# One timetable for two attention layers: a modulation row used six steps later, three weight fetches spread out, parts of k and q moved back

## The chip, the cores and the metric

The kernel runs on one core of a Trainium2 chip. The core has five engines with a queue each: TensorE (PE: matrix products and transposes, PEld its weight loads), VectorE (DVE), ScalarE (ACT), GpSimd (POOL) and SyncE (SP, which here only starts transfers). Instructions of a queue run in the order in which they were recorded; engines wait for one another by semaphores. Transfers between HBM and the on-chip memory (SBUF) are started from SP's and POOL's queues. The results of products are laid down in PSUM. The metric is the device time of one execution in microseconds (us).

## The reference

Two adaLN layers act on x, 8 batches of 512 tokens with 256 features. `c` gives each layer and batch six rows sa, ca, ga, sb, cb, gb (ga and gb are kept away from zero). Layer 0 has an attention of two branches, linear and windowed, and a feed-forward that mixes each token with the one before. Layer 1 has causal attention with rotary positions (rope) in 16 heads of 16 features, and a gated feed-forward with ternary weights.

```python
x = L0_attn_x
sa, ca, ga, sb, cb, gb = rows(L0_c, L0_wmod)
x = x + ga * L0_attn(layernorm(x) * (1 + ca) + sa)   # [linear | window 64] @ Wout, + its input
x = x + gb * L0_ffn(layernorm(x) * (1 + cb) + sb)    # sigmoid(xr Wr) * (relu(xk Wk)^2 Wv)
sa, ca, ga, sb, cb, gb = rows(L1_c, L1_wmod)
Q, K, V = (layernorm(x) * (1 + ca) + sa) @ w_qkv     # 16 heads of 16
Q, K = rope(Q), rope(K)                              # per head: x*cos + [-x2, x1]*sin
x = x + ga * (softmax(causal(Q K^T / 4)) V @ w_proj + b_proj)
h = layernorm(x) * (1 + cb) + sb
h = silu(w1 h * s1) * (w2 h * s2)                    # 256 -> 1024
h = gelu(h1 h * t1); h = gelu(h2 h * t2)             # 1024 -> 1024, twice
x = x + gb * (w3 h * s3)                             # 1024 -> 256
```

## The kernel before

**One timetable.** The attention of both layers and layer 0's feed-forward are not loops that run one after the other. Every small piece of work is a function that is entered in a list `plan` with a time: `when(time, what)` for layer 0, whose batch b starts at 20b (times after 169 are pressed together by 0.8), and `when1(time, what)` for layer 1, whose batch b starts at 24b; one of its steps is 0.603 of the list's unit once it has got going, and takes 2.33 us on the chip in the steady stretch. At the end the list is sorted by time and its functions are called under a manual schedule. So the order of the instructions on each engine is the order of the times, and nothing moves them afterwards: an instruction that waits holds up all that stands behind it in its queue. Only after the timetable (from 1181 us on) comes layer 1's feed-forward, a loop over the eight batches.

**Layer 1, step by step.** A unit of attention is a batch b, a half c of the features (0 or 1), and a parity e of the heads; a unit has six steps. In a step, `step1` records the scores k, q of one unit (PE, L1102) and the weights qs, k of the unit eight steps behind it (PE, L1160), interleaved. `finish_step1` records what follows: the row maxima on DVE (`junk`, L1113), the exponential on ACT (`at`, L1171) and the causal cut on POOL (`affine_select`, L1175). Once a unit, the maxima are transposed (L1136) and added to q as qs (DVE, L1144), the weights are multiplied by the values (L1194), copied (`ys`), transposed (L1210) and divided by their sums. Products that are not scores share two PSUM buffers, `mm`; scores have three, `sc`.

**What prepares a batch** (`prepare1(b)`). The batch's x is fetched, normalised (`normed`: statistics and `better` on DVE, the inverse root `rr` as two ACT instructions L286 and L287, the normalised rows L318), transposed (L986) and modulated into hT by ACT (L993). `rotation` makes k and q for half c: a product (PE L1012), its copy `flat` (ACT L1018), a swap of halves `rot` (DVE L1022), three POOL operations (L1027: rot times sine, flat times cosine, flat plus rot), and `apart` (ACT L1034), which writes the two head parities e of k or q from flat, each with the other parity's lanes zeroed. `values_of` makes the values (PE L1070).

**The fold of ga.** `fold(i)` prepares the output projection of a batch: fold(0) fetches the row ga as `bc`, a tile of 128 x 256, over SP (`mod_rows`, L189) into a pool with one buffer; fold(1) multiplies the projection's weights by it (`wps`, L973) and the row by the bias (`bc`, L974); fold(2) and fold(3) add that to the two halves of x (L977). All four products and sums are POOL's. The results are needed when `project_out(b)` multiplies by wps (PE L1252) at 24b + 42.45 and adds into x (L1262). Before, the folds stand at steps 49, 52, 53, 54 for batch 1, and at 24b + 6.5, 9.5, 10.5, 11.5 from batch 2 on (54.5, 57.5, 58.5, 59.5 for batch 2).

**bring(4)** at step 48.2 closes layer 0's memory, opens the pool of the feed-forward's weights, and fetches wproj, bproj and the scales over SP, and w1T, w2T and w3T, 1 MB each, over POOL's queue (L894), one behind the other. `look(m)` fetches raw halves of the weights (512 KB) over SP at 50 + 6m; DVE tests their low bits 5.6 steps later. 

**Layer 0's last batch.** `finish(b)` ends a batch of layer 0. It normalises x a second time as `hr` (root, `better`, four rows; for the last batch, 7, on ACT), transposes it (PE L741), and runs the small feed-forward (mixing on POOL and DVE, keys L165, `relu` on ACT, `ka` on DVE, L654 the product). At the time when batch 7 does this, layer 1's first units are already under way. Layer 0's own attention uses `at` and `aw` on ACT (L485, L561), selects on POOL (L489, L571), linear values on PE (L614) and copies of them (`ys`, L648).

Of the kernel before, what the change touches and what calls it, by code (L numbers as in the profile page):

```python
# [10 lines left out]
FR = mybir.dt.float32r  # L11
# [6 lines left out]
P = 128  # L18
B, T, D = 8, 512, 256
H, HD = 16, 16  # L20
NTB = T // P
NC = D // P
NG = 4
DH = 1024
NF = DH // P
# [5 lines left out]
def bcast(ap, shape, axis):  # L31
    return ap.unsqueeze(axis).to_broadcast(list(shape))
# [3 lines left out]
def adaln_two_layers_kernel(ctx: ExitStack, tc: tile.TileContext, t, out):  # L36
    nc = tc.nc
# [3 lines left out]
    def load(pool, name, shape, src, eng=None):  # L41
        dst = pool.tile(list(shape), FP, name=name, tag=name)
        (eng or nc.sync).dma_start(out=dst, in_=src)
        return dst
# [141 lines left out]
    def mod_rows(pool, b, first, n, bufs=2):  # L186

        bc = pool.tile([P, n, D], FP, name="bc", tag="bc", bufs=bufs)
        nc.sync.dma_start(out=bc, in_=mod_dram[b, first : first + n, :].partition_broadcast(P))  # L189
        return bc  # L190
# [4 lines left out]
    with ExitStack() as lctx:  # L195
# [43 lines left out]
        for h0 in (0, 64):  # L239
            first, later = wmask[h0 : h0 + 64, 0, :], wmask[h0 : h0 + 64, 1, :]  # L240
            nc.gpsimd.affine_select(
                out=first, in_=first, pattern=[[-1, P]], compare_op=ALU.is_ge, fill=-1e30, base=0, channel_multiplier=1
            )
            nc.gpsimd.affine_select(
                out=later, in_=later, pattern=[[-1, P]], compare_op=ALU.is_ge, fill=-1e30, base=WIN, channel_multiplier=1
            )
            nc.gpsimd.affine_select(
                out=later, in_=later, pattern=[[1, P]], compare_op=ALU.is_ge, fill=-1e30, base=0, channel_multiplier=-1
# [25 lines left out]
        def when(time, what):  # L274
            plan.append((min(time, END0) + STEP0 * max(time - END0, 0.0), len(plan), what))

        def when1(time, what):
            slow = min(max(time, 0.0), END1)
            plan.append((20 * B + 0.6 + slow + STEP1 * (time - slow), len(plan), what))
# [397 lines left out]
        def finish(b):  # L677

            t0 = 20 * b
# [43 lines left out]
            for j, ats_ in ((0, (34.6, 34.95)), (2, (35.45, 35.85))):  # L723
# [5 lines left out]
                when,  # L729
                lambda: xs0[b],  # L730
                [t0 + i for i in (35.6, 35.8, 36.28, 36.29)],
                t0 + 36.5,
                [t0 + 37.4 + 0.15 * j for j in range(NTB)],
                "hr",
                b == B - 1,
            )
# [100 lines left out]
        for m in range(2 * B):  # L837
            t0 = 10 * m
# [13 lines left out]
        for b in range(B):  # L852
            prepare(b)
            finish(b)
# [5 lines left out]
        def bring(i):  # L860
            if i == 0:
                got1["wqkv"] = wp.tile([P, NC, 3 * D], FP, name="wqkv", tag="wqkv")
                nc.sync.dma_start(out=got1["wqkv"], in_=t["L1_attn_w_qkv"].rearrange("(k p) n -> p k n", p=P))
            elif i == 1:
                got1["rope"] = fm.tile([P, 2, T], FP, name="rope", tag="qm", bufs=2)
                nc.sync.dma_start(out=got1["rope"][:, 0, :], in_=t["rope_cos"])
                nc.sync.dma_start(out=got1["rope"][:, 1, :], in_=t["rope_sin"])
            elif i == 2:


                cmask = got1["cmask"] = fm.tile([P, T], FP, name="cmask", tag="cat0", bufs=2)
                nc.gpsimd.memset(cmask, 0.0)
                diag = cmask[:, T - P : T]
                nc.gpsimd.affine_select(
                    out=diag, in_=diag, pattern=[[-1, P]], compare_op=ALU.is_ge, fill=-4e9, base=0, channel_multiplier=1
                )
            elif i == 3:

                home = [rp.tile([P, 2, T], FP, name="home", tag="aw", bufs=4) for _ in range(2)]
                got1["wproj"], wps[0] = (home[0][:, i, :].rearrange("p (k n) -> p k n", k=NC) for i in range(2))  # L880
                got1["bproj"], got1["bc"] = (home[1][:, 0, i * D : (i + 1) * D] for i in range(2))
                nc.sync.dma_start(out=got1["wproj"], in_=w_proj)
                nc.sync.dma_start(out=got1["bproj"], in_=t["L1_attn_b_proj"].partition_broadcast(P))
                nc.sync.dma_start(out=got1["bc"], in_=mod_dram[0, 4, :].partition_broadcast(P))
            else:
                only0.close()
                fpool = ctx.enter_context(tc.tile_pool(name="ffn_w", bufs=1, side="right"))
                lp = got1["lp"] = only1.enter_context(tc.tile_pool(name="only1", bufs=1, side="right"))
                got1["wproj"] = load(lp, "wproj", [P, NC, D], w_proj)
                got1["bproj"] = load(lp, "bproj", [P, D], t["L1_attn_b_proj"].partition_broadcast(P))  # L890

                for name, n, cols in (("w1T", NC, DH), ("w2T", NC, DH), ("w3T", NF, D)):
                    dst = full[name] = fpool.tile([P, n, cols], FR, name=name, tag=name)
                    nc.gpsimd.dma_start(out=dst, in_=t[name].rearrange("(k p) n -> p k n", p=P))  # L894
                for name in ("w1_s_cols", "w2_s_cols", "h1_s_cols", "h2_s_cols"):
                    full[name] = load(fpool, name, [P, NF], t[name])
                full["w3_s"] = load(fpool, "w3_s", [P, D], t["L1_ffn_w3_s"].partition_broadcast(P))
                full["x0"] = fpool.tile([P, NTB, D], FP, name="x0", tag="x0")
                full["low"] = fpool.tile([P, 22], FP, name="low", tag="low")
                full["flag"] = fpool.tile([1, 1], I32, name="flag", tag="flag")  # L900

        w_proj = t["L1_attn_w_proj"].rearrange("(k p) n -> p k n", p=P)
        only1, full = ExitStack(), {}
        for i, at in enumerate((146.2, 150.0, 157.0, 171.5)):
            when(at, lambda i=i: bring(i))
        when1(48.2, lambda: bring(4))


        raws = [
# [29 lines left out]
        def prepare1(b):  # L939

            t0 = 24 * b
# [24 lines left out]
            def fold(i):  # L966
                if i == 0:
                    held["bc"] = mod_rows(got1["lp"], b, 4, 1, 1)[:, 0, :] if b else got1["bc"]
                    if b:
                        wps[b] = got1["lp"].tile([P, NC, D], FP, name="wps", tag="wps", bufs=2)  # L970
                elif i == 1:
                    bc = held["bc"]
                    nc.gpsimd.tensor_tensor(wps[b], got1["wproj"], bcast(bc, [P, NC, D], 1), ALU.mult)  # L973
                    nc.gpsimd.tensor_tensor(bc, bc, got1["bproj"], ALU.mult)  # L974
                else:
                    h = xs1[b][:, 2 * i - 4 : 2 * i - 2, :]
                    nc.gpsimd.tensor_tensor(h, h, bcast(held["bc"], [P, 2, D], 1), ALU.add)  # L977

            at = (31.0, 49.0)[b] if b < 2 else t0 + 6.5
            for i in range(4):  # L980
                when1(at + (0.0, 3.0, 4.0, 5.0)[i], lambda i=i: fold(i))

            def by_features(c):
                ps = mm.tile([P, T], FP, name="mm", tag="mm")
# [67 lines left out]
            for c, which, at, begin, then, turn, last in (  # L1052
                (0, "k", -11.55, 152.50, 153.0, (153.3, 153.6, 154.2, 154.8), (156.0, 156.3)),
                (0, "q", -8.55, 153.50, 154.1, (155.0, 155.4, 156.0, 156.6), (157.9, 158.2)),
                (1, "k", 0.45, 156.70, 157.2, (157.5, 158.0, 158.6, 159.2), (160.3, 160.8)),
                (1, "q", 3.45, 157.70, 158.3, (159.9, 160.2, 160.8, 161.4), (162.2, 162.7)),
            ):
                if b == 0:
                    rotation(c, which, when, (begin, begin), then, turn, last)
                else:  # L1060
                    at += t0
                    turn = [at + i for i in (2.1, 2.4, 3.3, 4.2)]
                    near = b == 1 and at < 30.0
                    rotation(c, which, when1, (at, at + (0.05 if near else 1)), at + (0.5 if near else 1.6), turn, (at + 5.3, at + 6.1))
# [17 lines left out]
            for j, at in ((0, t0 + 6.45), (2, t0 + 9.45)):  # L1082
                if b == 0:
                    at = (6.7, 8.7)[j // 2]
# [219 lines left out]
        for b in range(B):  # L1304
            prepare1(b)
            project_out(b)
            for m in range(3 * b, min(3 * b + 3, len(raws))):
                at = 50 + 6 * m
                when1(at, lambda m=m: look(m))
                for i in range(2):  # L1310
                    when1(at + 5.6 + i, lambda m=m, i=i: low_bits(m, i))
# [212 lines left out]
```

## Time and profile before

| what | value |
|---|---|
| time, 3 runs | 1867.52 us median (1866.74 to 1873.74) |
| profiled execution | 1871.11 us, its span 1869.4 us |
| mean granted PE clock | 0.976 |
| PE busy | 1765.4 us, 94% |
| DVE busy | 1080.4 us, 58% |
| ACT busy | 895.6 us, 48% |
| POOL busy | 718.0 us, 38% |
| moved by DMA | 65.98 MB, mean 35 GB/s |

The page of the profile shows one execution. Busy shares are averages over stages with different limits. The timetable ends near 1181 us; behind it POOL is almost idle and PE runs the feed-forward's products. A row of the timeline gives the start, the duration, the engine, the line, the operation with its output and inputs and the shapes; the bracket says how long the engine was idle before it and which instruction released it. A row of a stretch gives, for each engine, busy time and the number of instructions, and then the granted clock of PE (1.00 is full speed), the share of DMA time and the rate.

### The profile page before, as it was taken

The page shows a single profiled execution, that of the slowest core. Times are in us where ns is not written, and L with a number is a line of the kernel's source. Part 1 is how long each engine was busy: PE and PEld are TensorE (multiplying, and loading weights), DVE is VectorE, ACT ScalarE, POOL GpSimd, SP SyncE. Part 2 cuts the span into 40 slices and gives each one's busy share as a digit, 9 for nine tenths or more (in the row PEclk, how much of TensorE's full clock was granted, in tenths as well). Part 3 has the DMA queues.
Part 4 walks back from the last instruction along what each step waited for, and adds up shares of the span by engine and source line. Part 5 has one row for each costly group of instructions (what it writes and reads, how often), then busy time and mean ns, then how long its engine had stood idle before and what let it go on. Part 6 is the DMA issues. An engine that isn't in the chain of part 4 may idle for free. (4 is left out here: it accounts for less than half of the span.)

```text
span 1869.4 us, 41160 instructions
## 1 busy us (share of the span) xinstructions
PE 1765.4 (94%) x16878; PEld 1198.6 (64%) x16878; DVE 1080.4 (58%) x3717; ACT 895.6 (48%) x1279; POOL 718.0 (38%) x1094
## 2 busy tenths in 40 slices
PE   3999999999999999989999999799999999999998
PEld 2456566665666654545545544588878888888877
DVE  3555664755646556568888885636363544636352
ACT  1676666766667544556766655322231322223221
POOL 4566856768575753565665653100000000000000
PEclk7999999999999998999999999899999999999999
DMA  4100001010000110042212110600000000000000
GB/s 148 44 2 14 20 24 36 5 36 26 19 18 31 39 31 11 24 108 75 66 49 69 51 49 24 217 0 15 1 26 26 1 26 1 26 1 26 1 15 13
DMA packets 41893, 65.98 MB, mean 35 GB/s; under 512 B 4056, under 2 KB 33368, under 8 KB 41696
## 3 DMA queue, kind: packets, MB, share of 16 engines
q1 hardware_dynamic: 36512, 47.02, 8.0%
q0 software_dynamic: 5184, 16.25, 2.8%
q8 instruction: 134, 2.20, 0.5%
q14 instruction: 63, 0.52, 0.1%
HBM read 50.63 MB, written 12.63 MB: 34 GB/s over the span
## 5 line engine op out<-in xcount | busy, mean ns | idle before, releaser
L1113 DVE CUSTOM_DVE_ANT_0 junk<-sc,cmask 128x256 bf16<-128x256 f32 (+3 forms) x512 | 225.4, 487 | 105.1 <-PE sc L1102 104.6
L1171 ACT ACTIVATE at<-sc 128x768 f32<-128x768 f32 (+1 forms) x192 | 168.9, 882 | 118.9 <-PE sc L1102 104.3
L571 POOL TENSOR_SCALAR_AFFINE_SELECT aw<-aw 64x512 f32<-64x512 f32 (+1 forms) x320 | 167.5, 550 | 101.9 <-ACT aw L561 95.8
L1102 PE MATMUL sc<-k,q 32*128 32x512 f32 (+3 forms) x1024 | 194.7, 477 | 4.9 <-ACT at L1171 4.9
L1370 PE MATMUL mm<-g2h,h 128*128 128x512 f32 x512 | 199.2, 389 | 0.0
L1370 PE MATMUL mm<-g2l,h 128*128 128x512 f32 x512 | 199.2, 389 | 0.0
L485 ACT ACTIVATE at<-sc 128x768 f32<-128x768 f32 (+1 forms) x192 | 164.2, 885 | 66.5 <-PE sc L474 65.9
L1370 PE MATMUL mm<-g1h,h 128*128 128x512 f32 x512 | 194.0, 389 | 0.0
L1370 PE MATMUL mm<-g1l,h 128*128 128x512 f32 x512 | 193.9, 389 | 0.0
L1160 PE MATMUL sc<-qs,k 32*128 32x384 f32 (+3 forms) x1024 | 190.6, 472 | 0.0
L1175 POOL TENSOR_SCALAR_AFFINE_SELECT at<-at 128x256 f32<-128x256 f32 x256 | 102.1, 411 | 193.8 <-ACT at L1171 193.4
L518 DVE CUSTOM_DVE_ANT_0 junk<-sc,wmask 128x128 bf16<-128x128 f32 x512 | 115.3, 286 | 80.4 <-PE sc L507 80.2
L489 POOL TENSOR_SCALAR_AFFINE_SELECT at<-at 128x256 f32<-128x256 f32 x256 | 103.9, 426 | 104.3 <-ACT at L485 103.3
L1427 ACT ACTIVATE row<-mm,h_s_cols 128x512 f32<-128x512 f32 x64 | 44.2, 690 | 188.0 <-PE mm L1370 188.0
L1160 PEld LDWEIGHTS sc<-qs,k 32*128 32x128 f32 x1024 | 82.0, 185 | 67.7 <-DVE maxima L1113 37.2
L1341 DVE CAST g3h<-row 128x512 fp32r<-128x512 f32 x64 | 27.3, 427 | 157.7 <-ACT row L1427 157.7
L1420 ACT ACTIVATE row<-mm,h_s_cols 128x512 f32<-128x512 f32 x64 | 43.5, 689 | 152.4 <-PE mm L1370 152.4
L1414 ACT ACTIVATE sg<-mm,w_s_cols 128x512 f32<-128x512 f32 x64 | 44.2, 691 | 144.8 <-PE mm L1370 88.8
L1370 PEld LDWEIGHTS mm<-g1h,h 128*128 128x128 f32 x512 | 96.1, 188 | 20.2
L1370 PEld LDWEIGHTS mm<-g1l,h 128*128 128x128 f32 x512 | 96.1, 188 | 20.1
L1370 PEld LDWEIGHTS mm<-g2h,h 128*128 128x128 f32 x512 | 96.1, 188 | 20.0
L1370 PEld LDWEIGHTS mm<-g2l,h 128*128 128x128 f32 x512 | 96.1, 188 | 19.9
(223 smaller groups left out, 3970.3 us busy)
## 6 DMA issues: line engine op xcount, KB each, us to landing
x_mid<-x SPq DMA_DIRECT2D x16, 512.0 KB, 3.2
x<-x_mid POOLq DMA_DIRECT2D x9, 512.0 KB, 4.3
x<-in_L_attn_x_dram SPq DMA_DIRECT2D x8, 512.0 KB, 4.5
raw<-in_h1T_dram SPq DMA_DIRECT2D x8, 512.0 KB, 3.5
raw<-in_h2T_dram SPq DMA_DIRECT2D x8, 512.0 KB, 3.5
h<-in_h1T_dram POOLq DMA_DIRECT2D x8, 512.0 KB, 7.7
h<-in_h2T_dram POOLq DMA_DIRECT2D x8, 512.0 KB, 10.0
out_dram<-tmp SPq DMA_DIRECT2D x16, 256.0 KB, 2.2
```

The source lines that it names most:

```text
L485: nc.scalar.activation(at, ps[:, :, :o], AF.Square, scale=0.5)
L489: nc.gpsimd.affine_select(out=d, in_=d, pattern=[[0, 2], [1, P]], compare_op=ALU.is_ge, fill=0.0, base=0, channel_multiplier=-1,)
L518: nc.vector.tensor_tensor_reduce(junk, ps[:, i, ii * P : (ii + 1) * P], wmask[:, int(blk > 0), :], -1.0, BIG, ALU.add, ALU.min, maxima[:, ...
L571: nc.gpsimd.affine_select(out=d, in_=d, pattern=[[0, d.shape[1]], [sign, 64]], compare_op=ALU.is_ge, fill=0.0, base=0, channel_multiplier= ...
L1102: nc.tensor.matmul(ps[:, i, o : o + m], q[r, e, qb * P : (qb + 1) * P], k[r, e, :m], start=True, stop=True,)
L1113: nc.vector.tensor_tensor_reduce(junk[:, :m], ps[:, i, o : o + m], got1["cmask"][:, T - m :], -1.0, BIG, ALU.add, ALU.min, maxima[:, NTB * ...
L1160: nc.tensor.matmul(ps[:, i, o : o + m], k[r, e, kb * P : (kb + 1) * P], qs[r, kb * P : T], start=True, stop=True)
L1171: nc.scalar.activation(at, ps[:, :, :o], AF.Exp, scale=0.25)
L1175: nc.gpsimd.affine_select(out=d, in_=d, pattern=[[0, 2], [1, P]], compare_op=ALU.is_ge, fill=0.0, base=0, channel_multiplier=-1,)
L1370: nc.tensor.matmul(ps, w[:, k, col : col + P], part[:, k, :], start=(k == 0 and i == 0), stop=(k == n - 1 and i == len(parts) - 1),)
L1414: nc.scalar.activation(sg, pa, AF.Silu, scale=full["w1_s_cols"][:, f : f + 1])
L1427: nc.scalar.activation(row(f), ps, AF.Gelu, scale=full["h2_s_cols"][:, f : f + 1])
```

## The change

Four things move in the timetable; no instruction is added or dropped, and PE's order stays as it was.

1. Layer 0's batch 7: its second root moves from 36.5 to 37.0 of its times, and its four normalised rows from 37.4 to 37.6 and following.
2. w1T, w2T and w3T: their buffers are still made in bring(4), but the three transfers are entered singly at steps 62.9, 68.9 and 74.9.
3. Folds: batch 1 still fetches its row at 49 but uses it at 58, 59 and 60; batch 2 fetches at 61 and uses the row at 64, 65 and 66. From batch 3 on nothing changes. On SP the fetch for batch 2 thereby goes behind one raw half of the low-bit test.
4. Layer 1's batch 0, half 1: `apart` of k moves from 160.3 and 160.8 to 161.3 and 162.3, that of q from 162.2 and 162.7 to 163.3 and 164.3. On ACT the two copies ys of layer 0 then come ahead of the k parts, and the q parts fall between relu, aw and the copies of the features.

```diff
--- before.py
+++ after.py
@@ -729,8 +729,8 @@
                 when,
                 lambda: xs0[b],
                 [t0 + i for i in (35.6, 35.8, 36.28, 36.29)],
-                t0 + 36.5,
-                [t0 + 37.4 + 0.15 * j for j in range(NTB)],
+                t0 + (36.5 if b < B - 1 else 37.0),
+                [t0 + (37.4 if b < B - 1 else 37.6) + 0.15 * j for j in range(NTB)],
                 "hr",
                 b == B - 1,
             )
@@ -889,9 +889,8 @@
                 got1["wproj"] = load(lp, "wproj", [P, NC, D], w_proj)
                 got1["bproj"] = load(lp, "bproj", [P, D], t["L1_attn_b_proj"].partition_broadcast(P))
 
-                for name, n, cols in (("w1T", NC, DH), ("w2T", NC, DH), ("w3T", NF, D)):
-                    dst = full[name] = fpool.tile([P, n, cols], FR, name=name, tag=name)
-                    nc.gpsimd.dma_start(out=dst, in_=t[name].rearrange("(k p) n -> p k n", p=P))
+                for i, (name, n, cols) in enumerate((("w1T", NC, DH), ("w2T", NC, DH), ("w3T", NF, D))):
+                    full[name] = fpool.tile([P, n, cols], FR, name=name, tag=name)
                 for name in ("w1_s_cols", "w2_s_cols", "h1_s_cols", "h2_s_cols"):
                     full[name] = load(fpool, name, [P, NF], t[name])
                 full["w3_s"] = load(fpool, "w3_s", [P, D], t["L1_ffn_w3_s"].partition_broadcast(P))
@@ -904,6 +903,11 @@
         for i, at in enumerate((146.2, 150.0, 157.0, 171.5)):
             when(at, lambda i=i: bring(i))
         when1(48.2, lambda: bring(4))
+        for i, name in enumerate(("w1T", "w2T", "w3T")):
+            when1(
+                62.9 + 6 * i,
+                lambda name=name: nc.gpsimd.dma_start(out=full[name], in_=t[name].rearrange("(k p) n -> p k n", p=P)),
+            )
 
 
         raws = [
@@ -976,9 +980,9 @@
                     h = xs1[b][:, 2 * i - 4 : 2 * i - 2, :]
                     nc.gpsimd.tensor_tensor(h, h, bcast(held["bc"], [P, 2, D], 1), ALU.add)
 
-            at = (31.0, 49.0)[b] if b < 2 else t0 + 6.5
+            at = (31.0, 49.0, 61.0)[b] if b < 3 else t0 + 6.5
             for i in range(4):
-                when1(at + (0.0, 3.0, 4.0, 5.0)[i], lambda i=i: fold(i))
+                when1(at + (0.0, 9.0, 10.0, 11.0)[i] if b == 1 else at + (0.0, 3.0, 4.0, 5.0)[i], lambda i=i: fold(i))
 
             def by_features(c):
                 ps = mm.tile([P, T], FP, name="mm", tag="mm")
@@ -1052,8 +1056,8 @@
             for c, which, at, begin, then, turn, last in (
                 (0, "k", -11.55, 152.50, 153.0, (153.3, 153.6, 154.2, 154.8), (156.0, 156.3)),
                 (0, "q", -8.55, 153.50, 154.1, (155.0, 155.4, 156.0, 156.6), (157.9, 158.2)),
-                (1, "k", 0.45, 156.70, 157.2, (157.5, 158.0, 158.6, 159.2), (160.3, 160.8)),
-                (1, "q", 3.45, 157.70, 158.3, (159.9, 160.2, 160.8, 161.4), (162.2, 162.7)),
+                (1, "k", 0.45, 156.70, 157.2, (157.5, 158.0, 158.6, 159.2), (161.3, 162.3)),
+                (1, "q", 3.45, 157.70, 158.3, (159.9, 160.2, 160.8, 161.4), (163.3, 164.3)),
             ):
                 if b == 0:
                     rotation(c, which, when, (begin, begin), then, turn, last)
```

## The prediction

> **What bounds the kernel now.** I read the page's busy shares and chain, then busy time by 20-us stretches, then the timeline where PE falls short, engine by engine. In the page:
>
> ```profile
> span 1869.4 us, 41160 instructions
> PE 1765.4 (94%) x16878; PEld 1198.6 (64%) x16878; DVE 1080.4 (58%) x3717; ACT 895.6 (48%) x1279; POOL 718.0 (38%) x1094
> PE 33%; DVE 1%; DMA 1%; ACT 0%; issue 0%; ACTq 0%; SPq 0%
> ```
>
> PE bounds. The chain followed back covers only the feed-forward from 1181 us, which the change leaves alone, but all stages before it share PE's queue, so time that PE loses before 1181 is lost at the end, and only that time. The stretches with short PE time that touch the change (columns: stretch, sum, PE, PEld, DVE, ACT, POOL, granted clock, DMA share, GB/s):
>
> ```profile
> 640.00:660.00 20.00, 17.29 (x322) 9.97 (x323) 14.48 (x47) 12.04 (x18) 18.03 (x25) 0.94 0.01 2
> 720.00:740.00 20.00, 17.06 (x115) 7.66 (x115) 12.27 (x55) 13.22 (x24) 8.31 (x11) 0.81 0.00 1
> 820.00:840.00 20.00, 14.09 (x112) 7.56 (x104) 8.93 (x38) 8.04 (x11) 13.27 (x16) 0.83 0.68 181
> 840.00:860.00 20.00, 20.00 (x188) 9.97 (x188) 16.20 (x56) 11.84 (x18) 13.11 (x19) 1.00 0.23 65
> ```
>
> At 820 PE lacks 5.9 us and the clock is down, while DMA is at 0.68. The timeline there (start, duration, engine, line, what it waited for):
>
> ```profile
> 816.10 0.93 POOL L894 DMA_DIRECT2D w3T<-in_w3T_dram  x1
> 818.63 0.63 SPq L189 DMA_DIRECT2D bc<-mod_dram  x1
> 829.11 1.26 POOL L973 TENSOR_TENSOR wps<-wproj,bc 128x512 f32<-128x512 f32 x1 [3.64 <-DMA bc<-mod_dram]
> 831.86 1.26 POOL L1027 TENSOR_TENSOR flat<-flat,rot 128x512 f32<-128x512 f32 x1
> 833.16 0.82 ACT L1034 ACTIVATE k<-flat,hot,half 128x512 f32<-128x512 f32 x1 [5.62 <-POOL flat L1027]
> 834.70 2.08 PE L1070 MATMUL mm<-wqkv,hT 128*128 128x256 f32 x4 [5.91 <-ACT hT L993]
> ```
>
> So the row bc lands 10.4 us after its issue, POOL stands in the product wps behind it, the rotation's last addition stands behind that on POOL, `apart` (L1034) on ACT, then the copy hT, and PE.
>
> What an idle stretch of PE does to the clock, in windows of 3.41 us and the two that follow (same columns):
>
> ```profile
> 722.45:725.86 3.41, 2.11 (x14) 1.06 (x12) 3.13 (x13) 1.84 (x4) 1.43 (x2) 0.98 0.00 0
> 725.86:732.69 6.83, 6.83 (x32) 1.92 (x32) 4.48 (x19) 5.74 (x12) 3.38 (x5) 0.51 0.01 2
> 265.06:268.47 3.41, 2.32 (x64) 1.12 (x52) 1.31 (x10) 1.69 (x3) 1.86 (x3) 1.00 0.12 25
> 268.47:275.30 6.83, 6.71 (x113) 3.98 (x106) 5.39 (x22) 5.00 (x9) 4.01 (x6) 1.00 0.05 12
> ```
>
> A window with 62% PE is followed by 6.83 us at half clock, one with 68% is not. Those 6.83 us lose up to half, 3.4 us; between these shares lies the point. The Trainium skill (TensorE: Matmul & The Clock Gate, "Why this matters for your kernels") puts the drop after PE-idle gaps above some 3 us; here a window with 1.30 us of idle time was enough, so the row decides.
>
> **A. First weights out of step 48.2, row of batch 1 used at 58.** Removed from POOL at 814.64 to 817.03: three DMA issues (0.74, 0.74, 0.93). Removed from 829 to 838: wps 1.26, bc 0.72, two additions of 1.27; they go to steps 58 to 60, where the same four of batch 2 now lie (845.59 to 852.41, PE 20.00 of 20 there), so they cost nothing; the row's fetch stays at step 49, nine steps of 2.33 us before its use, twice its 10.4. Without the wait POOL does the two selects from 825.7, the rotated sum from 826.46 to 827.73, ACT k to 828.6 and hT to 829.4, so L1070 starts at 829.45 instead of 834.70: 5.25 us. The half clock of 834.70 to 838.2 goes too: 3.5/2 = 1.75. Sum **-7.0**. Bounds: -5.25 if a drop comes anyway; -7.6 if the 0.67 us left vanishes too.
>
> **D. What comes into its place: batch 2 at 64 to 66.** POOL is nearly full there with batch 3's rotation:
>
> ```profile
> 860.85 0.77 POOL L1175 TENSOR_SCALAR_AFFINE_SELECT at<-at 128x256 f32<-128x256 f32 x2 [0.30 <-ACT at L1171]
> 861.59 1.27 POOL L1027 TENSOR_TENSOR flat<-flat,rot 128x512 f32<-128x512 f32 x1
> 862.89 0.82 ACT L1034 ACTIVATE k<-flat,hot,half 128x512 f32<-128x512 f32 x1 [0.28 <-POOL flat L1027]
> ```
>
> New ahead of 861.59: the issue of w1T (0.74), wps 1.34 and bc 0.68 (start to start at 829.11), less what idle time of POOL takes up; by queueing the rows the sum flat+rot ends at 864.80 instead of 862.86, 1.94 later. ACT's k and the copy aT behind it go 1.96 later, and PE L1252, which at 864.23 already waits 0.36 us for aT, stands 2.3 us. The two additions (1.23 each) delay the next selects; with them PE loses **2.4** in all. A window with 2.3 us idle is past the 1.30 that dropped the clock: a full drop is 3.4, I take 3.0 since PE waits a little in it anyway: **+5.4**. Bounds: 0 (batch 3's rotation slides into POOL's gaps) to 2.4 + 3.4, and with a second stall at q's sum (868.38) 11.2. The fetch of bc at 61 moves on SP behind one raw half; it can start once batch 1's second addition frees its only buffer (852.4), and at the median landing of 3.4 us it is there at 855.8, before wps. The other two weight issues (0.74 and 0.93 on POOL at 68.9 and 74.9) meet gaps of POOL (2.63 idle before 873.11), at most 0.5 of the second in a rotation: 0. On the DMA engines each weight now runs alone; the raw halves of the check are used 5.6 steps, 13 us, after their issue, against 15.6 for the slowest landing in the full pile: 0, at most 0.5. The Trainium skill (DMA: Bandwidth & Descriptors, "Issuing engines are not separate DMA queues") says that transfers of SP and POOL run on the same engines and interleave; the 10.4 against 3.4 agrees.
>
> **B. Second norm of layer 0's last batch.** ACT's order at 720:
>
> ```profile
> 723.99 0.30 ACT L286 ACTIVATE rr<-mv,eps 128x4 f32<-128x4 f32 x1 [3.39 <-DVE mv L305]
> 724.43 1.01 ACT L1171 ACTIVATE at<-sc 128x1024 f32<-128x1024 f32 x1
> 725.49 1.91 PE L1102 MATMUL sc<-k,q 32*128 32x512 f32 x4 [0.98 <-ACT at L1171]
> ```
>
> The root stands ahead of the exponential, whose scores were there at 722.55. Moved behind it (and behind the second k and the other batch's root), the exponential ends 1.88 earlier and PE's 0.98 + 0.32 idle there go. What is late next: on DVE, qs (L1144) now runs at 725.8 to 726.5, ahead of the batch's normalisation; its product on PE waits 1.7 us, so I keep a clock drop. Then hr comes 1 us later (the last at 731.0) and L741 starts at 732.4 instead of 733.32: **-0.9**. Bounds: -4 (second drop of 739.5 gone, 3.1 more) to +1.3, if PE's wait for hr adds a stall of the size removed.
>
> **C. Parts of k and q, second half, batch 0.** ACT's order at 654:
>
> ```profile
> 654.04 1.52 ACT L1034 ACTIVATE k<-flat,hot,half 128x512 f32<-128x512 f32 x2 [4.39 <-POOL flat L1027]
> 655.47 1.05 ACT L648 COPY ys<-mm 128x512 f32<-128x512 f32 x2
> 656.09 3.22 PE L614 MATMUL mm<-at,vo 128*32 128x512 f32 x32 [2.06 <-ACT ys L648]
> ```
>
> The k parts wait for POOL ahead of ys, PE for ys. With ys first it is copied at 651.9 and L614 starts at 654.03: PE's 2.06 go. But POOL is busy without a break from 647 to 664.46, DVE nearly so, and PE then waits for these at 660.9 to 663.1. q's sum still ends at 664.46, relu now waits for it, starts 1.2 us earlier than its 665.74, and the following product at 665.8 instead of 667.68: -1.9 without a clock drop in the new gap, +0.6 with one (2.5 lost, as part of the slow stretch waits for DVE). The gap puts 2.1 idle us into one window, past the 1.30, so I take **+0.6**. Bounds -1.9 to +0.6.
>
> **Sum:** -7.0 + 5.4 - 0.9 + 0.6 = **-1.9**; A alone is read from rows, the others are queueing and the clock. The profiled execution took 1871.1 us (span 1869.4 + 1.7), 3.6 above the median of the runs; so 1869.2 for it and **1865.6** against 1867.5.
>
> **Rivals.** (1) The gaps that remain don't drop the clock, D is 2.4, and B's second drop goes: -7.0 + 2.4 - 4 - 1.9 = -10.5, 1857.0. For it: the 68% window without a drop. Against: 2.3 us idle is 33% busy. By the skill's 3-us rule no gap here but A's would drop it; the profile has a drop after 0.98 + 0.32 us. Chance 0.22. (2) Slower, by D alone: batch 3's q sum, which follows k's on POOL, is late too, PE stalls twice with two drops, 2.4 + 3.4 + 2.0 + 3.4 = 11.2, against -7.0 - 0.9 + 0.6: +3.9, 1871.4. It decides once D is above 7.3, that is once a second window falls under 62%. For it: POOL is busy 10.7 of the 13.3 us from 857.18 to 870.48; against: the other 2.6 are gaps that take up a late start. Chance 0.25. (3) The change doesn't do what it says, the stall only moves: bc is still late behind scales and raw halves, or the pile moves to steps 62 to 75: about -0.5, 1867. Against: bc has 21 us. Chance 0.08. The forecast: 0.45.
>
> **The numbers.** About 0.5% (9.3 us) is what a measurement of this kernel can tell from no change. Faster by more needs rival 1 nearly whole, 0.12; slower by more needs rival 2 with B and C at their ends too and another drop or two, 0.03; the rest 0.85. The range takes in both rivals: 1856.5 to 1871.5; the likeliest case alone holds 1861 to 1869.
>
> **What would show it.** A: no wait of POOL for bc near 829 and PE full from 820 to 840 but for 0.7 us. D: PE L1252 waiting 2 us for aT near step 66 and half clock after it; were PE full there, D is nothing and the time near 1858. B: no wait of ACT for the root at 720, but one of PE for qs. C: L614 without its 2.06, PE's gap after it. Wrong if the clock windows fall otherwise than I place them: each such drop is worth up to 3.4 us, as much as all else but A.

## The result and the profile after

The changed kernel takes 1864.38 us in the median (1861.98 to 1867.37) against 1868.51 for the kernel before (1866.74 to 1875.24): a ratio of 0.9973, 95% interval 0.996 to 0.9986, or 5.0 us less (2.6 to 7.5). The ratios here are those of the means; the medians differ by 4.1 us. In a later set of runs the changed kernel took 1866.28 against 1868.84, ratio 0.9983 (0.9973 to 0.9994). The prediction was 1865.6 with the range 1856.5 to 1871.5: less than 0.5%, towards faster, and so it came. Its terms did not all come so.

The page of the changed kernel's profile, span and busy times:

```profile
span 1863.4 us, 41160 instructions
PE 1762.1 (95%) x16878; PEld 1199.6 (64%) x16878; DVE 1084.3 (58%) x3717; ACT 893.7 (48%) x1279; POOL 715.8 (38%) x1094
```

The span is 6.0 us shorter than in the profiled execution of before. The same stretches of 20 us (columns: stretch, sum, PE, PEld, DVE, ACT, POOL, granted clock, DMA share, GB/s):

```profile
640.00:660.00 20.00, 19.20 (x351) 10.86 (x340) 15.04 (x54) 12.21 (x18) 17.97 (x27) 1.00 0.01 2
660.00:680.00 20.00, 16.83 (x126) 10.74 (x125) 13.23 (x47) 8.05 (x15) 9.06 (x11) 0.83 0.04 7
720.00:740.00 20.00, 16.09 (x120) 8.32 (x118) 13.73 (x57) 14.03 (x26) 8.74 (x12) 0.87 0.00 1
820.00:840.00 20.00, 19.44 (x192) 10.66 (x184) 13.62 (x52) 13.25 (x18) 13.71 (x19) 1.00 0.17 56
840.00:860.00 20.00, 17.72 (x152) 8.90 (x151) 16.66 (x64) 11.42 (x16) 16.25 (x23) 1.00 0.35 113
```

At 820 PE has 19.44 in place of 14.09 us, and the full clock. At 840, where it had 20.00, it has lost 2.28. At 640 and 660 a loss only changed places: PE has 1.91 more in the one and 2.31 less in the other, where before has 19.14. From line 911 on the changed kernel's line numbers are four higher than those of before.

PE's order is the same in both kernels, so the start of one and the same PE instruction can be compared between any two traces. The next table gives the time between the starts of two fixed PE instructions, for four stretches named after the prediction's parts, and for two that nothing in this study touches: the head (to 184 us of before) and the tail (1132 to 1204 of before). In before, C runs from 653.30, B from 720.81, A from 826.29 and D from 861.98.

| profiled execution of | head | C | B | A | D | tail |
|---|---|---|---|---|---|---|
| before | 176.0 | 28.74 | 32.62 | 16.81 | 14.92 | 71.5 |
| changed | 177.7 | 28.50 | 31.27 | 9.72 | 18.87 | 69.6 |
| changed, second trace | 175.0 | 29.71 | 29.87 | 9.72 | 18.90 | 66.7 |
| e1 weights alone | 177.8 | 29.66 | 32.02 | 13.03 | 14.90 | 68.3 |
| e2 folds alone | 176.6 | 29.16 | 32.08 | 9.71 | 18.22 | 68.1 |
| e4 norm and parts | 175.4 | 29.41 | 29.84 | 17.69 | 14.92 | 67.6 |
| e5 norm alone | 177.8 | 29.67 | 29.82 | 17.43 | 14.91 | 67.6 |
| e6 parts alone | 175.3 | 29.45 | 30.43 | 17.31 | 14.91 | 67.6 |
| e7 folds and weights | 174.5 | 29.45 | 31.84 | 9.71 | 14.90 | 73.1 |
| e3 changed, batch 2 at 70 | 178.1 | 28.45 | 31.24 | 9.72 | 14.92 | 72.8 |
| e8 the same again | 180.9 | 29.76 | 30.40 | 9.71 | 14.92 | 66.9 |
| e11 the same, third | 175.4 | 30.01 | 30.52 | 9.71 | 14.90 | 69.0 |

Read the columns down. A and D are sharp: they fall into a few values to the hundredth. The untouched head spreads over 6.4 us and the tail over 6.4. They are the longer the more half clock (a granted clock of 0.50) an execution has there, 30.7 to 47.8 us in the head and 10.2 to 23.9 in the tail. That makes single times of one kernel differ by several us, and a pair of traces a poor measure of the whole. So D, and A where no half clock falls into it, are read from any trace, B and C from the mean over several, and the total from the times.

The first place, in the changed kernel (start, duration, engine, line, what it waited for):

```profile
825.69 1.28 POOL L1031 TENSOR_TENSOR flat<-flat,rot 128x512 f32<-128x512 f32 x1
827.01 0.81 ACT L1038 ACTIVATE k<-flat,hot,half 128x512 f32<-128x512 f32 x1 [0.28 <-POOL flat L1031]
827.73 0.76 ACT L997 ACTIVATE hT<-mm,modf 128x512 f32<-128x512 f32 x1
828.54 1.13 PE L1074 MATMUL mm<-wqkv,hT 128*128 128x256 f32 x4 [0.56 <-ACT hT L997]
```

POOL goes from the selects straight to the rotated sum, ACT's k waits 0.28 in place of 5.62 us, and PE 0.56 in place of 5.91. The second place:

```profile
850.50 0.74 POOL L909 DMA_DIRECT2D w1T<-in_w1T_dram  x1
852.87 1.26 POOL L977 TENSOR_TENSOR wps<-wproj,bc 128x512 f32<-128x512 f32 x1
854.21 0.73 POOL L978 TENSOR_TENSOR bc<-bc,bproj 128x256 f32<-128x256 f32 x1
855.62 1.26 POOL L1031 TENSOR_TENSOR flat<-flat,rot 128x512 f32<-128x512 f32 x1
856.92 0.81 ACT L1038 ACTIVATE k<-flat,hot,half 128x512 f32<-128x512 f32 x1 [2.19 <-POOL flat L1031]
858.25 1.13 PE L1256 MATMUL mm<-wps,aT 128*128 128x256 f32 x4 [2.28 <-ACT aT L1246]
```

The fold of batch 2 stands ahead of batch 3's rotated sum, and PE waits 2.28 us for aT.

### The profile page after: what moved, and what is told of

Its sections match the earlier page's. It is cut to its first block, busy times and chain, and to the rows that moved or that the text cites. A ratio compares the mean times of both kernels' runs of the same rounds, so it can differ in the third digit from the quotient of the medians.

```text
span 1863.4 us, 41160 instructions
## 1 busy us (share of the span) xinstructions
PE 1762.1 (95%) x16878; PEld 1199.6 (64%) x16878; DVE 1084.3 (58%) x3717; ACT 893.7 (48%) x1279; POOL 715.8 (38%) x1094
```

## The experiments

### The parts of the first place: e1 and e2

e1 takes only the weights' fetches apart:

```diff
-                for name, n, cols in (("w1T", NC, DH), ("w2T", NC, DH), ("w3T", NF, D)):
-                    dst = full[name] = fpool.tile([P, n, cols], FR, name=name, tag=name)
-                    nc.gpsimd.dma_start(out=dst, in_=t[name].rearrange("(k p) n -> p k n", p=P))
+                for i, (name, n, cols) in enumerate((("w1T", NC, DH), ("w2T", NC, DH), ("w3T", NF, D))):
+                    full[name] = fpool.tile([P, n, cols], FR, name=name, tag=name)
...
+        for i, name in enumerate(("w1T", "w2T", "w3T")):
+            when1(
+                62.9 + 6 * i,
+                lambda name=name: nc.gpsimd.dma_start(out=full[name], in_=t[name].rearrange("(k p) n -> p k n", p=P)),
+            )
```

> The kernel before with only w1T, w2T and w3T fetched singly at 62.9, 68.9 and 74.9; all folds where they were. Theory: the pile of 3 MB is what delays batch 1's row. Without it the row lands in 3.4 to 6 us, before POOL wants it at 825.5, and POOL's wait of 3.64 us is gone; but wps, the row's product and the two additions (4.5 us) still lie inside batch 2's rotation, so the rotated sum ends near 829.5, hT near 831.1, and PE still stands some 2.3 us there, as it does after the change at batch 3. Expected: 3.6 us less than before, 5 to 6 with the half-clock stretch gone, so less than the 7.3 that the whole change gains there; w1T's issue adds under 0.8 us at batch 3. Rival: the row is late for a reason of its own (SP's queue, the broadcast read); then it still lands after 10 us, POOL waits 3.6 us as before, and the time is that of before.

Measured: ratio 0.9992 (0.9979 to 1.0005), 1866.58 against 1867.12. In the trace the row of batch 1 lands in 4.9 us in place of 10.4, and POOL has no wait for it. The timeline of e1, POOL and PE:

```profile
825.89 1.27 POOL L1031 TENSOR_TENSOR flat<-flat,rope 128x512 f32<-128x512 f32 x1
827.12 1.27 POOL L977 TENSOR_TENSOR wps<-wproj,bc 128x512 f32<-128x512 f32 x1
829.88 1.27 POOL L1031 TENSOR_TENSOR flat<-flat,rot 128x512 f32<-128x512 f32 x1
832.72 1.85 PE L1074 MATMUL mm<-wqkv,hT 128*128 128x256 f32 x4 [2.23 <-ACT hT L997]
```

So the pile of 3 MB does delay the row, and the rival falls. But with the fold still inside the rotation, PE waits 2.23 us, the clock is half for 3.41 us behind that wait, and A shrinks by 3.78 us only (16.81 to 13.03). D is 14.90: w1T's issue inside batch 3's rotation costs nothing by itself. In the times the gain of 3.8 does not stand out of its interval (-3.9 to +0.9 us).

e2 moves only the folds:

```diff
-            at = (31.0, 49.0)[b] if b < 2 else t0 + 6.5
+            at = (31.0, 49.0, 61.0)[b] if b < 3 else t0 + 6.5
             for i in range(4):
-                when1(at + (0.0, 3.0, 4.0, 5.0)[i], lambda i=i: fold(i))
+                when1(at + (0.0, 9.0, 10.0, 11.0)[i] if b == 1 else at + (0.0, 3.0, 4.0, 5.0)[i], lambda i=i: fold(i))
```

> The kernel before with only the folds moved (batch 1 used at 58 to 60, batch 2 fetched at 61 and used at 64 to 66); the three weights stay together at 48.2. Theory: the row may land as late as before (10 us), nobody waits for it, and batch 2's rotation has POOL for itself: PE's 5.9 us at 828 fall to 0.7, the whole 7 us of that place. At batch 3 the cost remains but without w1T's issue of 0.74: PE waits some 1.6 us for aT in place of 2.28. Sum: 7.3 - 3 = some 4.5 us less than before. Rival: the pile delays something else that is needed, a raw half or a scale, and a new wait for it shows between 815 and 840; then less than half of the 7 us is gained.

Measured: ratio 0.9989 (0.9977 to 1.0001), 1865.44 against 1867.12. The row again lands after 10.4 us, and nobody waits: A is 9.71, all that the whole change has there. D is 18.22, with PE waiting 2.04 us for aT where I had expected 1.6, and half clock for 3.41 us behind it. The folds alone do both, the gain and the loss; taking the weights apart adds nothing to A. 7.1 - 3.3 = 3.8 us less by the stretches; the times, from 4.3 less to 0.2 more, allow it but do not show it.

### The second place mended: e3

```diff
-                when1(at + (0.0, 9.0, 10.0, 11.0)[i] if b == 1 else at + (0.0, 3.0, 4.0, 5.0)[i], lambda i=i: fold(i))
+                when1(at + (0.0, 9.0, 10.0, 11.0)[i] if b in (1, 2) else at + (0.0, 3.0, 4.0, 5.0)[i], lambda i=i: fold(i))
```

> The changed kernel with batch 2's fold used at 70, 71 and 72 (fetch still at 61), between its two neighbours' rotations, where POOL has gaps of 1.2 to 1.9 us between selects. Theory: the fold inside batch 3's rotation costs the 3.7 us that the two traces differ by from 858 to 873; moved out, PE's wait of 2.28 us for aT falls below 1 (w1T's issue is still there), and the kernel takes 3 to 3.7 us less than the changed one, some 8 less than before. Rival: the four POOL operations fill the selects' gaps at 866 to 876, where PE has 0.2 us of slack at most; then the wait appears there as one of PE for POOL's select or ACT's exponential, and the time is that of the changed kernel.

Measured: ratio 0.9944 (0.9923 to 0.9964), 1858.85 against 1867.12. It was run twice more, since its first times spread over 10 us:

> The changed kernel with batch 2's fold at 70, 71 and 72, a second time and with more rounds, as its four executions spread over 10 us. Theory: without the collision 3 to 4.5 us less than the changed kernel, 7 to 9 less than before. Rival: the first result was its executions' luck with the clock (its profiled one took as long as the changed kernel's); then some 4 to 5 less than before.

> The kernel with batch 2's fold at 70 to 72 and no idle product, as the measure for the two runs before, on the same chip: half clock near 738; by theory it takes 2 to 3 us more than the one with full-array products and the same as the one with small ones; 8 to 9 less than before.

These gave 0.9949 (0.9931 to 0.9968) and 0.9951 (0.9937 to 0.9965), 1860.43 and 1860.54. Stretch D is 14.92 again. The stretches of e3 that answer to 840 to 880:

```profile
840.00:860.00 20.00, 19.63 (x167) 9.98 (x164) 17.80 (x68) 12.60 (x19) 15.39 (x23) 1.00 0.36 112
860.00:880.00 20.00, 20.00 (x185) 9.83 (x187) 17.77 (x59) 12.96 (x19) 13.99 (x21) 1.00 0.43 136
```

The wait that was 2.28 us, and where the fold now lies on POOL:

```profile
856.84 1.13 PE L1256 MATMUL mm<-wps,aT 128*128 128x256 f32 x4 [0.37 <-ACT aT L1246]
866.10 1.26 POOL L977 TENSOR_TENSOR wps<-wproj,bc 128x512 f32<-128x512 f32 x1
```

PE is full where the fold now lies, in the gaps between the selects. Beside the changed kernel on the same chip it took 5.7 us less (1860.54 and 1866.28), somewhat more than the 3.95 of stretch D. It beats both kernels, by some 9 us the one before.

### The two orders on ACT: e4, e5, e6, e7

e4 has the other two parts of the change, and none of the folds and weights:

```diff
-                t0 + 36.5,
-                [t0 + 37.4 + 0.15 * j for j in range(NTB)],
+                t0 + (36.5 if b < B - 1 else 37.0),
+                [t0 + (37.4 if b < B - 1 else 37.6) + 0.15 * j for j in range(NTB)],
...
-                (1, "k", 0.45, 156.70, 157.2, (157.5, 158.0, 158.6, 159.2), (160.3, 160.8)),
-                (1, "q", 3.45, 157.70, 158.3, (159.9, 160.2, 160.8, 161.4), (162.2, 162.7)),
+                (1, "k", 0.45, 156.70, 157.2, (157.5, 158.0, 158.6, 159.2), (161.3, 162.3)),
+                (1, "q", 3.45, 157.70, 158.3, (159.9, 160.2, 160.8, 161.4), (163.3, 164.3)),
```

> The kernel before with only the orders on ACT changed: batch 7's second root and rows later, k's and q's parts of batch 0 later. Theory: the parts gain nothing, since POOL and DVE hold the stretch up to 665 and PE's 2.06 us of waiting come back as a wait for the divided rows (0.2 us less in all between 650 and 670), and the root gains 1.1 us. Expected: 1 to 1.5 us less than before, within the noise of the times, to be read in the trace by how much earlier the same PE instruction starts. Rival: the parts' 2.06 us are kept where the clock falls otherwise; then 3 us less.

Measured: ratio 1.0017 (1.0005 to 1.0028), 1869.14 against 1867.12: slower, where I had 1 to 1.5 less. So each was run alone, e5 with the first pair of lines and e6 with the second, and e7 as e3 without both:

> The kernel before with only batch 7's second root and rows moved later. The two orders on ACT together took 2.0 us more than before in the median, while their profiled execution had PE ahead of before by 0.2 to 1 us from 735 to 839; so the executions differ in where the clock falls, and one of the two orders must cost. Theory 1, the root costs: it turns PE's two short waits (0.98 and 0.32 us) into one of 1.71 us for qs, which puts the clock down in more executions; then this kernel takes 1 to 3 us more than before. Theory 2, the parts cost: then this one takes 1 us less, as the rows had it.

> The kernel before with only the parts of k and q of batch 0 moved later. By theory 1 (the root costs) this takes as long as before, within 1 us: PE's 2.06 us of waiting for ys come back as 2.3 us of waiting for the divided rows. By theory 2 (the parts cost) it takes 1 to 3 us more: the new wait comes later, at the small feed-forward's first products, and the half clock after it falls on more of PE's work.

> The kernel before with the weights fetched singly and the folds of batch 1 at 58 to 60 and of batch 2 at 70 to 72; the orders on ACT as before. By theory 1 or 2 it should beat the kernel with those orders changed too (the next run) by what they cost, some 2 us, and before by 9 to 10: the 7.3 of the first place and nothing lost at batch 3. If the orders on ACT cost nothing here, both take the same, some 8 less than before.

Measured: e5 0.9986 (0.9972 to 1.0001), e6 1.0004 (0.9991 to 1.0018), e7 0.9969 (0.9957 to 0.9982). Theory 1 falls, as the root alone does not cost. For theory 2 there is no more than a sign (e6, +1.6 us in the median, within its interval), and e7 speaks against it: without the orders it took 3 us more than with them (1863.51 and 1860.43 on the same chip, with ratio intervals that just overlap), not less. By the stretches B is 30.42 in the mean over the seven executions of the table with the later root and 31.80 over the five without: 1.4 us gained. C is 29.33 over the seven with the later parts and 29.34 over the five without: nothing. Why e4's times are above before's is open: its profiled execution, at 1866.56 the fastest of its ten, has nothing in these stretches that costs 2 us, and the others of the ten have no trace. One part can be read from the traces: A is 0.5 to 0.9 us longer in e4, e5 and e6 than in before (17.3 to 17.7 against 16.81). It is not the row, which lands 2.5 to 2.8 us behind the start of A in all four. All four have 6.83 us of half clock there. But in before only 3.65 us of it lie behind the end of PE's wait, at L1070, and the rest inside the wait, where nothing is lost; in e4, e5 and e6 5.65, 5.83 and 5.34 lie behind it. Half of the difference, 0.8 to 1.1 us, accounts for the longer A.

### What halves the clock: e9 and e10

The changed kernel has PE idle for 2.28 us at batch 3 and no half clock behind it. e2 has a shorter gap, 2.04, and half clock. One window of 3.41 us and the two that follow, of the changed kernel:

```profile
854.25:857.66 3.41, 1.73 (x15) 0.73 (x12) 2.18 (x13) 1.22 (x3) 3.41 (x5) 1.00 0.44 157
857.66:864.49 6.83, 5.85 (x40) 3.00 (x44) 6.26 (x13) 3.58 (x7) 6.83 (x9) 1.00 0.01 1
```

and one window and the next of e2:

```profile
855.86:859.27 3.41, 1.37 (x11) 0.42 (x9) 2.39 (x13) 1.46 (x4) 3.41 (x5) 1.00 0.01 2
859.27:862.68 3.41, 3.41 (x12) 2.40 (x16) 1.73 (x6) 1.85 (x4) 3.41 (x6) 0.50 0.00 0
```

PE's busy share is 0.51 here without a drop, while in before 0.62 and even 0.77 had one. Over the traces another measure separates the windows: the columns that each product moves, weighted by the part of the 128x128 array that it uses (a product over 32 rows and 128 columns counts a quarter), summed over the window. Each float32 product leaves two records and a transpose one, and a record that crosses the window's edge counts by its part inside. In the changed kernel's window the scores and weights between 854.84 and 855.97 (8 records of 512 columns at a quarter: 1,024), the transposes L1214 (4 x 128 = 512) and the end of L1243 (some 150) make some 1,680. In e2's, which began 0.5 us later in this order of work, behind most of the transposes, it is 1,197. To test it, e9 fills the two gaps that precede the half clock near 738 in every trace so far, e10 does the same with a sixteenth of the array:

```diff
+        def idle_product(s):
+            if s == 22:
+                early_mm.append(mm.tile([P, T], FP, name="mm", tag="mm"))
+            ps = early_mm[0]
+            nc.tensor.matmul(ps[:, 0:256], ident, got1["cmask"][:, 0:256], start=True, stop=True)
...
+                    if i == 0 and s in (22, 23) and mats is todo[0][0]:
+                        idle_product(s)
```

(e10: `ps[0:32, 0:256], ident[0:32, 0:32], got1["cmask"][0:32, 0:256]`; both on top of e3.)

> The kernel with batch 2's fold at 70 to 72, and two idle products that fill PE's gaps of 0.99 and 0.62 us near 736 and 738 (steps 22 and 23): each multiplies the 128x128 identity by 256 columns, 0.56 us, into a PSUM tile that the transposes behind overwrite. In the ten profiled executions so far the clock was half after every window of 3.41 us in which the columns moved by the products, each weighted by the share of the 128x128 array that it uses, came to less than some 1,510 (a full window holds some 3,100), and, with one exception, after no other; busy time alone does not separate them (0.50 without a drop, 0.77 with one). The window before 738 had 920 to 1,460 and dropped in all ten. Theory: the two products add up to 1,024; no half clock near 738 here, and PE is some 2.5 us earlier from 750 on. Rival: what counts is PE's idle time; then the same.

> As the run before, but the two idle products use 32 rows and 32 columns of the array: the same columns, the same time, the same place. Theory (array-weighted work counts): they add 2 x 256 x 1/16 = 32 to the window; the clock is half near 738 as in all ten executions, and the time is that of the kernel without the products. Rival (idle time counts): PE is busy in the window as in the run before, and the half clock is gone here too.

Measured: in e9 the clock is never half between 669 and 1126; in e10 it is half at 740.90. Two successive windows of e9:

```profile
733.59:737.01 3.42, 3.06 (x32) 1.91 (x30) 1.20 (x8) 2.59 (x5) 2.50 (x3) 1.00 0.01 2
737.01:740.42 3.41, 3.41 (x23) 1.92 (x22) 3.22 (x12) 2.54 (x3) 2.61 (x6) 1.00 0.00 0
```

The same of e10:

```profile
737.49:740.90 3.41, 2.89 (x31) 1.75 (x30) 1.20 (x8) 2.58 (x5) 2.52 (x3) 1.00 0.01 2
740.90:744.31 3.41, 3.41 (x18) 2.08 (x16) 2.54 (x11) 1.54 (x2) 2.50 (x5) 0.50 0.00 0
```

PE is busy 0.90 and 0.85 of the windows, with the same products in the same places but for the array's part; weighted columns are some 1,980 and 1,299. The one has the full clock, the other not. So idle time alone is not what counts, and the rival falls; each of the two kernels has one trace. Stretch B is 28.64 in e9, 29.83 in e10 and 30.52 in e11 without either. In the times it stays small: 1860.09, 1864.15 and 1860.54 (ratios 0.9957, 0.9972, 0.9951 with overlapping intervals), so e9 is no faster than e11 by its times, where 2 to 3 us less were expected, and e10, expected to equal e11, has a median 3.6 us above it, which stays unexplained. That the products save time was not shown, only that the full-array ones hold the clock.

### The changed kernel once more

> The changed kernel once more, beside its mended form on the same chip: 3.7 us more than that one by the two traces, 5 by the medians so far; PE again waits 2.3 us for aT at batch 3. The clock is half behind that wait only where the window's weighted columns fall below 1,510; the profiled execution of the change had 1,683 there and no half clock, the folds alone had 1,197 and had it.

Its second trace has D at 18.90 and again no half clock there; the times are those given at the top.

## Why the prediction was right, and where not

**What bounds.** Right: PE's idle time and half clock before 1181 are what the end moves by.

**A, -7.0.** Right: 16.81 to 9.72 is -7.1. The row was late by the pile (10.4 us with it, 4.9 without it in e1), and POOL, ACT and PE stood behind it as read from the chain of rows. The prediction put it under both edits together; e2 shows that the folds alone bring all of it, e1 that the weights alone bring 3.8. That the size fits to 0.1 us is in part luck: with the half clock placed as in e4, e5 and e6 the gain would be 7.6 to 8.0.

**D, +5.4.** The mechanism and the first wait were right: PE waits 2.28 us against 2.3, on the instruction named, L1252 of before, and is 1.9 us later behind it, as worked out. The size was not: the stretch costs 3.95. Two steps behind the first wait failed, in opposite directions.

The first is "A window with 2.3 us idle is past the 1.30 that dropped the clock: a full drop is 3.4, I take 3.0". There was no drop in either trace of the changed kernel. By the measure of e9 and e10 the window held some 1,680 weighted columns in the one, and no window there held fewer than some 1,990 in the other. By that measure it hangs on where the edge of the window falls, and so it is in part luck: e2 has the drop. Even there the drop did not add to the rest, for e2's D of 18.22 is shorter than the changed kernel's 18.87 without one.

The second is the delay that follows, "with them PE loses 2.4 in all", which leaves some 0.5 us behind the first wait. Measured are 2.05. Of these 0.46 come at L1198, which waits for POOL's select at 863.30. The rest runs along a way that the prediction did not have, here in the changed kernel and then in before:

```profile
861.62 1.26 POOL L1031 TENSOR_TENSOR flat<-flat,rope 128x512 f32<-128x512 f32 x1
861.70 1.21 DVE L293 TENSOR_SCALAR rt<-rt 128x4 f32<-128x4 f32 x1
863.29 1.22 DVE L310 SCALAR_TENSOR_TENSOR off<-mv,rr 128x4 f32<-128x4 f32 x1
864.55 1.09 ACT L318 ACTIVATE h<-x,off,rr 128x256 f32<-128x256 f32 x2 [2.60 <-DVE off L310]
```

```profile
867.48 0.17 DVE L293 TENSOR_SCALAR rt<-rt 128x4 f32<-128x4 f32 x1
867.88 0.17 DVE L310 SCALAR_TENSOR_TENSOR off<-mv,rr 128x4 f32<-128x4 f32 x1
868.08 1.10 ACT L318 ACTIVATE h<-x,off,rr 128x256 f32<-128x256 f32 x2 [0.15 <-DVE off L310]
```

The five small DVE operations of the next batch's normalisation, L291 to L310, take 4.0 us from the first start to the last end in place of 1.4. L293 ends 0.02 us behind the POOL operation that runs beside it. ACT's normalised rows wait 2.60 us for their result, and the next exponential stands behind these rows. Both traces of the changed kernel have this; in the other twelve L293 and L310 take 0.16 to 0.17. The chain is read from the rows, and no run tests it by itself. That e3 takes all 3.95 back shows that the fold's place is the cause of both waits.

**B, -0.9.** -1.35 between the two traces, -1.4 in the means. The wait moved to qs as foretold. The changed kernel, ACT and PE:

```profile
723.10 1.02 ACT L1175 ACTIVATE at<-sc 128x1024 f32<-128x1024 f32 x1 [1.92 <-PE sc L1106]
724.73 0.28 ACT L286 ACTIVATE rr<-mv,eps 128x4 f32<-128x4 f32 x1
727.01 0.59 PE L1164 MATMUL sc<-qs,k 32*128 32x384 f32 x2 [1.71 <-DVE qs L1148]
```

The root now stands behind the exponential, and PE waits 1.71 us for qs where 1.7 was worked out. The second half clock, at 738, came as in before. What the clock adds can be told apart: among the traces with 10.24 us of half clock in this stretch, the four with the later root have 30.86 in the mean and the three without 31.98, so 1.1 us belong to the root. The rest is that three others with the later root have only 3.41 us of half clock; whether the root brings that too is open.

**C, +0.6.** -0.24 between the two traces, 0.0 in the means. The wait for ys went (2.06 us), and came back:

```profile
664.13 1.08 PE L654 MATMUL mm<-ident,ys 128*128 128x128 f32 x4 [2.37 <-DVE rows L670]
665.13 0.60 ACT L788 ACTIVATE relu<-mm 128x512 f32<-128x512 f32 x1 [6.63 <-POOL flat L1031]
```

2.37 us for the divided rows, and relu behind POOL's sum for q, both foretold. Two sizes failed. The product that the prediction put 1.9 us earlier, at 665.8 in place of 667.68, comes 1.2 earlier, counted from the start of the stretch. The half clock lay from 657.44 to 664.27 in before and lies from 663.11 to 669.94 here, so it moved and none was added; it takes back 1.0 us by the end of the stretch, where 2.5 was put.

**The sum.** -7.1 + 3.95 - 1.4 + 0 = -4.5, against ratios that give -5.0 and -3.2; I had -1.9, by 1.5 too much on D, 0.5 too little on B and 0.6 too much on C. D's 1.5 is what two errors leave of each other, 3.0 too much for the clock and some 1.6 too little for the delay. That the forecast of 1865.6 lies 1.2 us from the measured median is luck in part: the kernel before, measured anew, took 1.0 us more than the 1867.5 that the forecast starts from, and the change brought more than the -1.9. The profiled pair's 6.0 holds 1.7 lost in the untouched head and 1.9 gained in the tail.

**The rivals.** (1), without drops behind the gaps that remain, was right for D's clock, but D cost 3.95 and not 2.4, B's second drop stayed, and the -1.9 at C did not come. By the rule of the Trainium skill (TensorE: Matmul & The Clock Gate, "Why this matters for your kernels") neither D nor B would have had a drop; the changed kernel's D agrees (2.28 us, none), and the runs disagree for B (gaps of 0.99 and 0.62 us, half clock in every trace without the full-array products) and for e2's D (2.04 us). (2), two stalls and two drops at batch 3, did not come: behind the first stall there are short waits, 2.05 us in all, and no drop. (3), that the stall only moves: the raw halves and scales delayed nothing, and of A nothing came back.

## What to carry to other kernels

Where instructions run in a written order, a wait for a late transfer can be taken out by moving its consumer or by making the transfer faster. Here the first brought more, since the consumer's own work left the crowded stretch too (7.1 us against 3.8). Then look at what the consumer's new place holds: its length on its engine has to fit the gaps there, and small operations of another engine beside it can become late as well. Here a shift by six more steps, from 64 to 70, was worth 4 to 6 us, as much as the whole change. In these traces the array-weighted work around a gap of PE tells whether the clock falls behind it, better than the gap's length does. Effects of a us or two can't be read off one pair of traces while untouched stretches differ by six.

## What was not expected of the hardware

The clock's windows. Over the 14 traces, between 105 and 1170 us and leaving out windows already at half clock, 70 windows of 3.41 us were followed by half clock and 4,199 were not. A bound of 1,510 weighted float32 columns misplaces three of them (a drop at 1,524, none at 1,428 and 1,488, so not every window below the bound drops), while the best bound on PE's busy share misplaces 30. Windows with a drop had busy shares up to 0.85, windows without one down to 0.42. By their own best bounds, columns without a weight misplace 64, and columns weighted by the rows of the array alone 26. The bound was set on the first ten traces; in the four of e9 to e12 it misplaces one window. A window filled by full-array float32 products holds some 3,100 such columns (4 records of 256 in the 1.13 us of L1256 above), so the bound lies near half. In this measure scores over 32 rows count a quarter of their columns. That fits a drop behind gaps of 0.99 and 0.62 us among such scores near 738, and none behind the 2.28 us of the changed kernel. It is a rule fitted to the traces of one kernel and tested by e9 and e10; no run here shows how the chip itself counts.

Small DVE operations beside POOL's. In all 14 traces L291 of batch 3's stretch, an operation on 128x4 elements, starts beside an operation of POOL on 128x512 and ends 0.01 to 0.02 us behind it, after 0.64 to 1.15 us. L293 and L310 take 1.21 and 1.22 us where they start beside one, in the two traces of the changed kernel, and 0.16 to 0.17 in the twelve others.
